# A four-layer graph kernel on one core: layer 3's product in two levels of Strassen with its factors streamed from DRAM, layer 2's sums kept in PSUM

## The chip, the core and the metric

The kernel runs on one core of a Trainium2 chip. The metric is device time in microseconds (us) of one launch; less is better. TensorE (PE) does the matrix products, VectorE (DVE), ScalarE (ACT) and GpSimd (POOL) the elementwise work, and every DMA is issued on SyncE's queue (SP).

## The reference

`x` is 128 graphs of 64 nodes with 512 features, in float32; `adj` is 128 matrices of 64x64. Four residual layers follow each other, `x = x + layer(relu(layernorm(x)))`. Cut to what is computed (h is the normed input, per graph):

```python
# layer 0: two hypergraph convolutions, 512 -> 1024 -> 512, with M = a 64x64 matrix made of adj
z = layer_norm(relu(rd * (M @ h) @ W1.T + b1)); y = rd * (M @ (z @ W2.T)) + b2 + h
# layer 1: attention weights from two dot products; one 512x512 product
out = (A @ h) @ w
# layer 2: attention, with q = h Wq, k = h Wk, v = h Wv (+ biases)
weight = adj * exp(q @ k.T); out = (weight / weight.sum(2)) @ v
# layer 3: three-hop diffusion; transition is 64x64
H = 0; Xk = h
for k in range(3):
    H = H + Xk @ Wk[k] + bk[k]
    Xk = transition @ Xk
out = relu(H)
```

Layer 3 is thus one product of the row block [h, T h, T T h] (1536 wide) with the three 512x512 matrices `Wk` under each other.

## The kernel before

**Tiles.** A group is 8 graphs, that is four tiles of 128 rows (t = 0 to 3); there are 16 groups. The first half of the run takes all groups through layers 0 and 1 and stores the result to a DRAM scratch (`xm`, L809). The second half loads it again (L344) and takes all groups through layers 2 and 3.

**The order.** Nothing is issued where it is written. Each helper (`pe`, `dve`, `act`, `pool`, `dma`) puts an operation with an engine, an assumed cost, the buffers it reads and writes and a priority into a graph (`Graph.op`, L52). `Graph.run` (L82) then plays the graph through with one clock for each engine and a fixed latency, picks on each engine the operation that can start first (the lower priority number among equals), gives out the buffers of `SLOTS` and `TWO` (L185 to L202), and at the end issues all operations in the order of the planned start. So the order on every engine is fixed when the program is built, and operations of several groups and layers are woven into each other. The priorities are the sum of a group's period (`PERIOD1`, `PERIOD2`), a shift for each part (`AT`, L281) and `step(us)` times a stretch for the layer (`STRETCH`, L280). Where the plan leaves PE idle for over 0.5 us, `fill` (L1011) puts in matmuls of ones.

**Strassen.** The large products are done two tiles at a time, as a 2x2 block product with seven block multiplications (Winograd's form). `strassen` (L589) makes the combinations of the left factor on DVE (`comb`, L599), `combine` and `combine_hT` (L384, L403) those of the weights, once. `seven` (L568) issues the seven products: product 1 is copied from PSUM to SBUF by ACT (L575), DVE adds products 6 and 7 to it (L577, L579), and products 2, 5, 4 and 3 are summed with these by an `emit` function of the layer. A float32 matmul is two passes on PE, so each matmul of the program is two records in the profile.

- Layer 2 (`layer2`, L811): the normed tiles are transposed to `hT`, DVE makes four combinations (L831), seven products of four 128x256 matmuls give q (with the product of Wq and Wk folded into one matrix `wg`), then logits (L879), exp, and seven more products give v; the biases of q and v are added by POOL (L866, L900) and DVE (L867, L902). L912 multiplies by the attention matrix, L918 adds to `x`.
- Layer 3 (`layer3`, L922): DVE and PE make the transition matrix and its square (L949, L959); for each pair of tiles (t0 = 0, 2) the left factor `a3` of 12 blocks is put together from a transposed h (L557) and the two products with the transition (L975, copied out by ACT at L980). Then `strassen` with 6 blocks of contraction and 256 columns: 42 matmuls of 128x256 for a pair, 84 for a group (PE at L607 with `wb_mem`). `emit_o` (L985) adds the bias on POOL (L989) and the result on DVE (L993, L994) and stores to `out` (L997).

The factors of `Wk` (all seven combinations) lie in SBUF for the whole second half, in `wb_mem` (10752 floats a partition), where `W2` and `w` lay in the first half; they are loaded (L1063) and combined (L393 to L396 with 1536 columns) at the change from the first to the second half.

Of the kernel before, what the change touches and what calls it, by code (L numbers as in the profile page):

```python
# [35 lines left out]
class Op:  # L36
    __slots__ = ("eng", "cost", "fn", "prio", "bufs", "npre", "succ", "ready", "seq")


class Graph:  # L40
# [11 lines left out]
    def op(self, eng, cost, fn, r=(), w=()):  # L52
        o = Op()
        o.eng, o.cost, o.fn, o.prio = eng, cost, fn, self.prio + self.shift
# [27 lines left out]
    def run(self, slots, after, fill):  # L82
# [22 lines left out]
        while left:  # L105
# [23 lines left out]
            if o.eng == "PE" and gap > 0.5 and since <= at["PE"]:  # L129
                fills.append((o.seq, slots["ps"][i], gap))  # L130
# [8 lines left out]
            end = t + o.cost + self.LATENCY[o.eng]  # L139
# [28 lines left out]
def tile_adj_preln_d4(  # L168
# [25 lines left out]
        ([("tmp", [P, D], 4), ("mB", [P, T, C + 1], 1)], [("s3", [P, 3, 6, P], 1)]),  # L194
        ([("z", [P, DH], 2)], [("hT", [P, KD, T * P], 1)]),
        ([("rT", [P, KH, P], 3)], [("vu", [P, 2, D + 1], 2), ("tt", [P, T, 2, C], 2)]),
        ([("s2", [P, 3, 4, P], 1), ("s1", [P, 3, 2, P], 2)], [("a3", [P, 3 * KD, P], 2)]),
        ([("y", [P, D], 2)], [("qT", [P, 2, 2 * P], 2)]),
        ([("mT", [P, KD, P], 3)], [("a3", [P, 3 * KD, P], 1)]),
        ([("row", [P, D], 4)], [("sh", [P, 4, 2, 2 * P], 1)]),  # L200
        ([("wa", [P, D], 1)], [("q", [P, D], 1)]),
    ]  # L202
# [29 lines left out]
    WB = const.tile([P, 10752], F32, name="wb_mem")  # L232
# [6 lines left out]
    w2_sb = view(WB, 0, KH, D)  # L239
    w2_x = view(WB, 4096, 3 * 4, D // 2).rearrange("p (i c) o -> p i c o", i=3)  # L240
    w_sb = view(WB, 7168, KD, D)
    w_x = view(WB, 9216, 3 * 2, D // 2).rearrange("p (i c) o -> p i c o", i=3)
# [4 lines left out]
    w3_sb = view(WB, 0, 3 * KD, D)  # L247
    w3_x = view(WB, 6144, 3 * 6, D // 2).rearrange("p (i c) o -> p i c o", i=3)

# [21 lines left out]
    def dma(kb, fn, r, w, issue=0.34):  # L271
        return G.op("SP", max(kb / 380.0, issue), fn, r, w)

    def quad(b):
        return b.t.rearrange("p (c k) -> p c k", c=4)

    FILL = 0.75


    STRETCH, PERIOD1, PERIOD2 = (2.11, 6.43, 4.5, 0.21), 79.8, 140.53  # L280
    AT = {  # L281
        "x0": -1458.56, "apart": 58.27, "w1": -1207.06, "b1": -1268.61, "w2": 312.2, "w": -214.25, "c1": 103.95,
        "l0": -1592.46, "c2": -560.69, "l1": 125.29, "c": 849.04, "g0": -1279.86, "g1": -1456.39, "g2": -589.08,
        "g3": -1259.16, "g": -1258.76, "bq": 321.93, "l3": 56.2, "wg": 1603.23, "w3": 387.13, "beg0": -72.8,
        "beg1": 73.58, "end00": 0.51, "end01": 19.09, "end11": -75.14, "new2": 31.64, "new3": 4.77, "end2": -39.58,
        "end3": -21.31, "load1": -108.19, "load2": 27.97, "m": 12.29, "h0": 9.53, "p0": 10.98, "z0": -29.14,
        "q0": 15.48, "y0": -518.61, "h1": -26.33, "p1": -22.59, "z1": -30.25, "q1": 4.48, "y1": -2.94, "s": -20.64,
        "t0": -25.67, "e0": -522.9, "t1": -42.32, "e1": -53.88, "hT": 8.77, "sh": 220.05, "lq": 8.14, "pt": -124.53,
        "v": 35.92, "pv": -915.5, "s3": 19.84, "tt": -865.12, "a0": 46.62, "b0": -371.48, "a1": 104.26, "b1_": 198.72,
# [46 lines left out]
    def load_group(g, src, apart=0.0):  # L336
        b = Buf("adj")
        dma(256, lambda: nc.sync.dma_start(b.t, adj[g]), [], [b])
        adjs[g] = b
        for t in range(T):  # L340
            xx = Buf("x")
            at, key = src(g, t)
            G.shift += apart
            dma(256, lambda xx=xx, at=at: nc.sync.dma_start(xx.t, at), key, [xx])  # L344
            xt[g, t] = xx
# [5 lines left out]
    def x_mid(g, t):  # L351
        return xmid[g, t], [("xmid", g, t)]
# [12 lines left out]
    load_w("w2", w2_sb, W2T)  # L365
    b2_b = load_row(b2)
    part("w")
    load_w("w", w_sb, w)
# [5 lines left out]
    bk3_b = const.tile([P, D], F32, name="bk3_b")  # L374
# [9 lines left out]
    def combine(name, w_, x_, kc, n, eng, olds=()):  # L384
# [7 lines left out]
        T1 = name + "T1"  # L392
# [38 lines left out]
    def setup_l0():  # L431
# [6 lines left out]
        pe(c_mm(512, KH), mm, ["gb2b", *wkeys("w2", 0, KH)], [p])  # L438
        act(0.6, lambda: nc.scalar.copy(row.t[0:1, :], p.t[0:1, :]), [p], [row])
        for c in range(KH):  # L440
            act(0.72, lambda c=c: nc.scalar.activation(w2_sb[:, c, :], w2_sb[:, c, :], AF.Copy, scale=gb2[:, 0, c:c + 1]), ["gb2g"], [("w2", c // 2)])
# [11 lines left out]
    def setup_l1():  # L453
        wa, a_b = Buf("col"), temp(a.partition_broadcast(P))
        for c in range(KD):
            dot(lambda c=c: w_sb[:, c, :], lambda: a_b.t, lambda c=c: wa.t[:, c:c + 1], [("w", c // 2), ("w", "given"), a_b], [(wa, c)])
# [36 lines left out]
    def setup_l3():  # L493
# [12 lines left out]
        dma(256, lambda: nc.sync.dma_start(bk3_b, bk3[0].partition_broadcast(P)), [], ["bk3"])  # L506
        for k in range(1, 3):
            b = temp(bk3[k].partition_broadcast(P))
            dve(0.69, lambda b=b: nc.vector.tensor_add(bk3_b, bk3_b, b.t), [b, "bk3"], ["bk3"])


# [39 lines left out]
    def transposed(src, ksrc, planes, back, kback, dst, kdst):  # L551
# [4 lines left out]
        dma(0, lambda: nc.sync.dma_start_transpose(u16(back()).rearrange("p (b r) -> p b r", r=P), u16(planes.t)), [planes], kback, 1.23)  # L556
        act(1.16, lambda: nc.scalar.copy(u16(dst()).rearrange("p c (k q) -> p c k q", q=2), u16(back()).rearrange("p (q c r) -> p c r q", q=2, c=KD)), kback, kdst)  # L557

    def proj(lhsT, rhs, p, r, first=True, last=True):
# [6 lines left out]
        pe(c_mm(512, k), mm, r if first else [*r, p], [p])  # L566

# [21 lines left out]
    def strassen(A, keys, B, kc, n, stag, emit):  # L589
# [11 lines left out]
        def prod(lhs, kl, b):  # L601
            rhs, kb = B[b]
# [18 lines left out]
    def scaled(dst, wdst, scale, ks, add, ka, p, u, v, n):  # L621
# [5 lines left out]
        dve(c_v(n, True), lambda: nc.vector.scalar_tensor_tensor(dst(), p.t[:, :n], scale(), add(), op0=ALU.mult, op1=ALU.add), [p, *ks, *ka], [wdst])  # L627

    def biased(dst, j, p, u, v, row, krow):
# [7 lines left out]
        dve(c_v(D // 2, True), lambda: nc.vector.tensor_add(dst.t[:, cols], p.t[:, :D // 2], add()), [p, ka], [(dst, j)])  # L637
# [494 lines left out]
```

## Time and profile before

| | |
|---|---|
| runs | 2374.16, 2375.67, 2378.42 us; median 2375.67 |
| profiled execution | 2372.54 us, of which the span of instructions is 2370.7 us |
| PE | busy 2343.9 us, 99% of the span, 12264 records |
| DVE | busy 1741.8 us, 73% |
| ACT | busy 1268.0 us, 53% |
| POOL | busy 955.9 us, 40% |
| DMA | 171.06 MB, 72 GB/s over the span |
| one group, first half (layers 0 and 1) | 71.7 us |
| one group, second half (layers 2 and 3) | 71.6 us (mean of nine) |

A line of the group table reads: source line, engine, operation, output from inputs, partitions by elements, count; then the busy time of all, the mean duration of one in ns, and the idle time ahead of them with what ended it. PE's matmuls are pipelined: a record lasts longer than the step from one start to the next, so the step is what a matmul costs in a dense stretch.

### The profile page before, as it was taken

The numbers are of one execution on the slowest core, as the hardware profiler recorded it, in microseconds if no ns is written. First come the engines' busy times: TensorE is split into PE (matmuls) and PEld (weight loads), VectorE is DVE, ScalarE is ACT, GpSimd is POOL, SyncE is SP. The second block draws the span as 40 slices with busy tenths as digits, with TensorE's granted clock in tenths as the row PEclk, the third lists the DMA queues.
The fourth block names the chain that finished last, engine by engine and source line by source line (L and its number), as shares of the span: only waits on it lengthen the run. The fifth ranks groups of instructions, "written<-read, shape, count | busy, mean of one in ns | idle before, by whom it ended". The sixth has DMA issues, their size and how long they took to land.

```text
span 2370.7 us, 34372 instructions
## 1 busy us (share of the span) xinstructions
PE 2343.9 (99%) x12264; PEld 1851.4 (78%) x12264; DVE 1741.8 (73%) x3798; ACT 1268.0 (53%) x1746; POOL 955.9 (40%) x1514
## 2 busy tenths in 40 slices
PE   9999999999999999999999999999999999999999
PEld 4677677776667776677788888888888888888887
DVE  7878778777778877777868566666666766667664
ACT  4566566566565676565745445444454444454422
POOL 6234555444555444555443323333323332323330
PEclk9999999999999999999999999999999999999999
DMA  7333233232232332232442322223222223222211
GB/s 259 79 80 60 53 69 69 72 80 54 54 74 65 76 73 48 67 69 70 125 120 59 76 66 60 68 49 72 73 63 69 55 56 78 70 63 63 52 37 41
DMA packets 336924, 171.06 MB, mean 72 GB/s; under 512 B 284656, under 2 KB 290672, under 8 KB 336752
## 3 DMA queue, kind: packets, MB, share of 16 engines
q1 hardware_dynamic: 336752, 168.86, 29.6%
q8 instruction: 96, 1.57, 0.3%
q14 instruction: 76, 0.62, 0.1%
HBM read 66.99 MB, written 34.70 MB: 43 GB/s over the span
## 4 chain that ended last, share of the span: by engine, by line
PE 85%; DVE 5%; DMA 4%; ACT 2%; issue 1%; POOL 1%; SPq 1%; DVEq 0%; ACTq 0%
PE ps L607 59%; PE ps L846 14%; PE ps L546 5%; PE ps L912 2%; PE ps L759 2%; PE ps L975 1%; PE ps L879 1%; DMA x<-xm 1%; DMA rw<-row 1%; DVE st L516 1%; DMA adj<-in_adj_dram 1%; POOL nm L524 0%; SPq L556 0%; DVE tmp_mB_s L599 0%; DVE o L381 0%
## 5 line engine op out<-in xcount | busy, mean ns | idle before, releaser
L537 ACT ACTIVATE h<-x,nm,rs 128x512 f32<-128x512 f32 x384 | 300.1, 810 | 402.6 <-POOL nm L524 369.9
L607 PE MATMUL ps<-wb_mem,s_s_a 128*128 128x256 f32 x2184 | 512.0, 380 | 1.0 <-DVE u L579 0.6
L607 PEld LDWEIGHTS ps<-wb_mem,s_s_a 128*128 128x128 f32 x2184 | 409.5, 190 | 74.7 <-issue 19.6
L518 POOL TENSOR_SCALAR rs<-mv 128x1 f32<-128x1 f32 x320 | 99.4, 311 | 494.8 <-DVE mv L517 479.3
L607 PE MATMUL ps<-wb_mem,tmp_mB_s 128*128 128x256 f32 x1152 | 262.5, 380 | 2.7 <-DVE tmp_mB_s L599 2.7
L607 PEld LDWEIGHTS ps<-wb_mem,tmp_mB_s 128*128 128x128 f32 x1152 | 218.1, 190 | 35.2 <-DVE tmp_mB_s L599 5.3
L607 PE MATMUL ps<-wa_mem,mT_a 128*128 128x512 f32 x512 | 238.8, 598 | 4.5 <-ACT mT_a L548 3.9
L607 PE MATMUL ps<-wb_mem,mT_a 128*128 128x256 f32 x1016 | 242.0, 380 | 0.0
L607 PE MATMUL ps<-wb_mem,rT_vu_tt 128*128 128x256 f32 x1024 | 238.3, 380 | 0.8 <-ACT rT_vu_tt L557 0.7
L607 PEld LDWEIGHTS ps<-wb_mem,rT_vu_tt 128*128 128x128 f32 x1024 | 192.4, 190 | 42.2 <-issue 14.0
L607 PEld LDWEIGHTS ps<-wb_mem,mT_a 128*128 128x128 f32 x1016 | 192.2, 190 | 31.8 <-issue 6.0
L516 DVE BATCH_NORM_STATS2 st<-x 128x6 f32<-128x512 f32 x256 | 173.5, 678 | 47.1 <-DMA x<-xm 42.1
L519 POOL TENSOR_TENSOR rs<-rs,mhalf 128x1 f32<-128x1 f32 x320 | 193.5, 605 | 26.4
L607 PEld LDWEIGHTS ps<-wa_mem,mT_a 128*128 128x128 f32 x512 | 97.8, 192 | 114.2 <-issue 103.2
L607 PE MATMUL ps<-wa_mem,s_s_a 128*128 128x512 f32 x384 | 180.6, 593 | 0.0
L989 POOL TENSOR_TENSOR u<-u,bk_b 128x256 f32<-128x256 f32 x96 | 76.1, 792 | 236.9 <-DVE u L579 168.3
L575 ACT COPY u<-ps 128x256 f32<-128x256 f32 (+1 forms) x160 | 72.7, 454 | 178.7 <-PE ps L846 106.9
L635 POOL TENSOR_TENSOR u<-u,row_sh 128x256 f32<-128x256 f32 x96 | 74.5, 784 | 227.8 <-DVE u L577 211.7
L734 ACT ACTIVATE z_hT<-z_hT 128x512 f32<-128x512 f32 x128 | 79.6, 627 | 156.2 <-DVE z_hT L627 156.2
L557 ACT COPY rT_vu_tt<-z_hT 128x1024 uint16<-128x1024 uint16 x128 | 147.2, 1160 | 15.7 <-DMA z_hT<-tmp_mB_s 15.3
L546 PEld LDWEIGHTS ps<-bd,h 128*128 128x128 f32 x1024 | 131.0, 192 | 26.3 <-issue 22.0
L524 POOL TENSOR_SCALAR nm<-mv,rs 128x1 f32<-128x1 f32 x320 | 136.1, 425 | 31.1
(174 smaller groups left out, 4303.7 us busy)
## 6 DMA issues: line engine op xcount, KB each, us to landing
x<-in_x_dram SPq DMA_DIRECT2D x64, 256.0 KB, 2.7
xm<-x SPq DMA_DIRECT2D x64, 256.0 KB, 2.1
x<-xm SPq DMA_DIRECT2D x64, 256.0 KB, 2.8
out_dram<-x SPq DMA_DIRECT2D x64, 256.0 KB, 2.1
adj<-in_adj_dram SPq DMA_DIRECT2D x32, 256.0 KB, 3.9
rw<-row SPq DMA_DIRECT2D x94, 64.0 KB, 2.6
wb_mem<-in_Wk_dram SPq DMA_DIRECT2D x6, 512.0 KB, 5.8
tmp_mB_s<-in_Wk_dram SPq DMA_DIRECT2D x8, 256.0 KB, 3.2
```

The costliest lines, as they stand in the source:

```text
L516: dve(0.69, lambda i=i: nc.vector.bn_stats(st.t[:, i, :], src(i)), [r[i]], [(st, i)])
L518: pool(0.32, lambda: nc.gpsimd.tensor_scalar_add(rs.t, mv.t[:, 1:2], EPS), [mv], [rs])
L519: pool(0.65, lambda: nc.gpsimd.tensor_tensor(rs.t, rs.t, mhalf, ALU.pow), [rs], [rs])
L524: pool(0.47, lambda: nc.gpsimd.tensor_scalar(nm.t, mv.t[:, 0:1], rs.t, -1.0, op0=ALU.mult, op1=ALU.mult), [mv, rs], [nm])
L537: act(0.82, lambda: nc.scalar.activation(h.t, xx.t, AF.Relu, bias=nm.t, scale=rs.t), [xx, nm, rs], [h])
L546: nc.tensor.matmul(quad(p)[:, c, :], h.t[:, c * P:(c + 1) * P], rhs(), start=True, stop=True)
L557: act(1.16, lambda: nc.scalar.copy(u16(dst()).rearrange("p c (k q) -> p c k q", q=2), u16(back()).rearrange("p (q c r) -> p c r q", q=2, c ...
L607: nc.tensor.matmul(p.t[:, :n], lhs()[:, c, :], rhs(c), start=first and c == 0, stop=c == kc - 1, skip_group_check=True)
L635: pool(0.75, lambda: nc.gpsimd.tensor_add(U.t[:, iv], U.t[:, iu], row()[:, cols]), [u, krow], [v])
L734: act(0.63, lambda: nc.scalar.activation(z.t[:, cols], z.t[:, cols], AF.Relu), [(z, j)], [(z, j)])
L846: nc.tensor.matmul(pair(p.t)[:, o, :], a, b, start=first and o == 0 and c == 0, stop=c == 1, skip_group_check=True)
L989: pool(0.88, lambda: nc.gpsimd.tensor_add(U.t[:, iv], U.t[:, u[1]], add()), [u, ka], [v])
```

## The change

1. **Layer 3's product** is taken for all four tiles of a group at once, as a 2x2 block product (Winograd's form) whose left blocks are pairs of tiles by half the features and whose seven multiplications are each done by a second level of seven: 7 x 7 products of three 128x128 matmuls, 147 for a group. The 49 factors of the weights are made on POOL in the first half (`setup_w3`, 21 pieces, one for each of the seven outer factors and three hops) and written to DRAM. In the second half each outer product loads its factors in two DMAs (four inner blocks, 768 KB, and three, 576 KB), 14 DMAs and 9408 KB for a group, into three buffers `wf`.
2. **Piling up in PSUM.** Each outer product runs in two PSUM banks (inner blocks 1, 2, 6, 5 in one, 7, 3, 4 in the other). Outer products 1, 6, 5, 3 add up in one chain of banks, 7, 4 in another; ACT copies the sum after each link to SBUF (`snapshot`, buffer `zz`), DVE adds in the other chain (`plus`), and POOL undoes the inner level with five adds (`emit`), then DVE does relu and the residual.
3. **Left factors.** DVE makes three inner combinations for each outer product (`xi`, 128x384), 21 for a group, and six outer ones (128x768), and four adds on h (128x256) ahead of the transposes.
4. **Layer 2** uses `chained` for `seven`: products 1, 6, 7, 4 pile up in one bank, 5 and 3 in another, ACT copies the sums out (for q with the bias), so that DVE's L577/L579 and POOL's L866 drop out there. The first half keeps `seven`.
5. **x in layer 2** is loaded a second time from `xm` for the residual, four DMAs of 256 KB more a group.
6. **Planner**: an operation can carry its own latency (3.2 us for transfers of the second half in place of 2.0), the fill threshold is 1.0 us in place of 0.5, and `STRETCH`, `PERIOD2` and most of `AT` have other values.

The core of the diff:

```diff
+    def chained(mul, U, n, emit, fifth=None, biased_by=None):
+        px, py, pz = (Buf("ps") for _ in range(3))
...
+        mul[1](px, True)
+        snap(px, (U, 0), 0)
+        mul[2](py, True)
+        emit(0, 0, py, (U, 0), (U, 0))
+        mul[6](px, False)
+        snap(px, (U, 1), 0)
+        mul[5](pz, True)
+        snap(pz, fifth)
+        mul[7](px, False)
+        snap(px, (U, 2), 1)
+        emit(1, 1, fifth, (U, 2), (U, 2))
+        mul[3](pz, False)
+        emit(0, 1, pz, (U, 1), (U, 1))
+        mul[4](px, False)
+        emit(1, 0, px, None, (U, 0))
...
+    def setup_w3(f, k, when):
...
+            b = Buf("wp")
+            dma(256, lambda: nc.sync.dma_start(b.t.rearrange("p (q n) k -> p q (n k)", q=2), src(i, j)), when, [b, *turn])
...
+            pool(1.3, lambda: sub(out.t, y.t, x_.t), [y, x_], [out])
...
+            pool(0.8, lambda: sub(R.t[:, 1:3], F.t[:, 1::2], F.t[:, 0:2]), [F], [R, *turn])
+            pool(0.53, lambda: sub(R.t[:, 0], F.t[:, 3], R.t[:, 1]), [F, R], [R])
+            pool(0.53, lambda: sub(R.t[:, 3], F.t[:, 2], R.t[:, 0]), [F, R], [R])
...
+            dma(256, lambda xx=xx, at=at: nc.sync.dma_start(xx.t, at), [*key, (PT, 0)], [xx, ("xo", g, t)], lat=LAT)
...
+                if t >= 2:
+                    dve(0.52, lambda hv=hv: nc.vector.tensor_add(hv()[:, 0], hv()[:, 0], hv()[:, 1]), [h], [h])
+                if t % 2:
+                    dve(0.52, lambda hv=hv: nc.vector.tensor_add(hv()[:, :, 0], hv()[:, :, 0], hv()[:, :, 1]), [h], [h])
...
+        def minus(y, x_, blk, kd):
+            for v in range(2):
+                dve(1.02, lambda v=v: nc.vector.tensor_sub(blk[v](), y[0][v](), x_[0][v]()), [*y[1][v], *x_[1][v]], [kd[v]])
...
+        def product(f, F, chain, first):
...
+            dve(0.6, lambda: sub(x2(), lo(B), lo(A)), [*ka, *kb], [(X, 0)])
+            dve(0.6, lambda: sub(x3(), hi(B), x2()), [*kb, (X, 0)], [(X, 1)])
+            dve(0.6, lambda: sub(x4(), hi(A), x2()), [*ka, (X, 0)], [(X, 2)])
...
+            for n in range(2):
+                w_, p, q = Buf("wf"), banks[chain][n], len(BLOCKS[n])
...
+                dma(q * 192, lambda n=n, w_=w_, q=q: nc.sync.dma_start(
+                    w_.t[:, :q].rearrange("p r k c -> p (r k c)"), fac[f - 1][n]), [("fac", f - 1, n, k, d) for k in range(3) for d in FACS[n]], [w_], lat=LAT)
...
+                        for k in range(3):
+                            nc.tensor.matmul(inner(p, q)[:, r, :], at()[:, k, :], w_.t[:, r, k, :], start=first and r == 0 and k == 0,
+                                             stop=k == 2, skip_group_check=True)
...
+        def emit(i, j, Z):
...
+            pool(0.84, lambda: add(z(0, 4, 3), z(0, 4, 3), bk3_b.t[:, 2 * j * P:2 * (j + 1) * P].rearrange("p (a b) -> p a b", a=2)), [(Z, 0), bk3_b], [(Z, 0)])
+            pool(0.92, lambda: add(z(1, 3), z(1, 3), cast(0)), [(Z, 0)], [(Z, 0)])
+            pool(0.92, lambda: add(z(0, 8, 7), z(3, 5), cast(2)), [(Z, 0), (Z, 1)], [(Z, 0), (Z, 1)])
+            pool(0.64, lambda: add(z(4, 5), z(7, 8), z(3, 4)), [(Z, 0), (Z, 1)], [(Z, 0), (Z, 1)])
+            pool(0.92, lambda: add(z(2, 4), z(5, 7), z(0, 8, 7)), [(Z, 0), (Z, 1)], [(Z, 0), (Z, 1)])
...
+        minus(S1, A00, S2[0], [k[0] for k in S2[1]])
+        product(1, A00, "X", True)
+        s0 = snapshot("X")
+        minus(A11, S2, A00[0], [k[-1] for k in A00[1]])
+        product(2, A01, "Y", True)
+        plus(s0, "Y")
+        emit(0, 0, s0)
+        product(6, S2, "X", False)
+        s1 = snapshot("X")
+        minus(A01, S2, A01[0], [k[-1] for k in A01[1]])
+        product(5, S1, "X", False)
+        s2 = snapshot("X")
+        product(3, A01, "X", False)
+        s3 = snapshot("X")
+        emit(0, 1, s3)
+        product(7, A00, "Y", True)
+        plus(s2, "Y")
+        emit(1, 1, s2)
+        product(4, A11, "Y", False)
+        plus(s1, "Y")
+        emit(1, 0, s1)
```

The order of the instructions that the planner gives out for the changed kernel can be listed without running it; the prediction uses this list for counts and for what stands next to what.

## Prediction

> **What bounds the kernel now.** I read the page's busy times first, then the slices and the chain of work that ended last, then windows of single groups of the second half.
>
> ```profile
> PE 2343.9 (99%) x12264; PEld 1851.4 (78%) x12264; DVE 1741.8 (73%) x3798; ACT 1268.0 (53%) x1746; POOL 955.9 (40%) x1514
> ...
> PE   9999999999999999999999999999999999999999
> ...
> PEclk9999999999999999999999999999999999999999
> ...
> PE 85%; DVE 5%; DMA 4%; ACT 2%; issue 1%; POOL 1%; SPq 1%; DVEq 0%; ACTq 0%
> PE ps L607 59%; PE ps L846 14%; PE ps L546 5%; PE ps L912 2%; PE ps L759 2%; PE ps L975 1%; PE ps L879 1%; DMA x<-xm 1%; DMA rw<-row 1%; DVE st L516 1%; DMA adj<-in_adj_dram 1%; POOL nm L524 0%; SPq L556 0%; DVE tmp_mB_s L599 0%; DVE o L381 0%
> ```
>
> PE is busy in every slice at the full clock, and 85% of the chain is PE, most of it L607, the Strassen products. So the end moves with PE's work, if the others keep it fed. How close they come is seen from three groups of the second half, cut at L959:
>
> ```profile
> core 0: us, PE busy (x) PEld busy (x) DVE busy (x) ACT busy (x) POOL busy (x), PEclk, DMA share, GB/s
> 1608.20:1679.50 71.30, 71.23 (x448) 62.07 (x444) 48.15 (x107) 33.91 (x47) 23.67 (x38) 1.00 0.28 65
> 1679.50:1751.70 72.20, 71.42 (x446) 61.91 (x442) 48.45 (x107) 33.73 (x47) 23.46 (x38) 1.00 0.27 65
> 1751.70:1823.30 71.60, 71.47 (x449) 62.16 (x445) 48.58 (x107) 34.31 (x48) 23.66 (x38) 1.00 0.29 65
> ```
>
> A group takes 71.6 us; PE waits 0.07, 0.78 and 0.13 us of it, a third of a microsecond on average. DVE is at 68%, ACT 47%, POOL 33%, DMA 28%. There is nothing to win by taking waits away, only by giving PE less work.
>
> **1. PE's work (the gain).** In the second half only layer 3's product changes for PE: 84 matmuls of 256 columns a group become 147 of 128 columns; in the list of instructions all other counts (layer 2, logits, L975) are the same. Each is two records: 168 become 294. The cost of a record is the step in a dense run. The nearest row for 128 columns with a new stationary operand each time is L546. From the timeline, two runs without gaps:
>
> ```profile
> 362.29 1.95 PE L546 MATMUL ps<-bd,h 128*128 128x128 f32 x16
> ...
> 1616.87 5.34 PE L607 MATMUL ps<-wb_mem,tmp_mB_s 128*128 128x256 f32 x24
> ```
>
> and from the groups by shape, the duration of one (in ns, the second number after the bar):
>
> ```profile
> L607 PE MATMUL ps<-wb_mem,tmp_mB_s 128*128 128x256 f32 x1152 | 262.5, 380 | 2.7 <-DVE tmp_mB_s L599 2.7
> ...
> L546 PE MATMUL ps<-bd,h 128*128 128x128 f32 x1024 | 131.9, 275 | 0.2 <-ACT bd L709 0.2
> ```
>
> A run lasts (n-1) steps and one duration: (1.95 - 0.275) / 15 = 0.1117 us for 128 columns, (5.34 - 0.38) / 23 = 0.2157 for 256. A group has 168 x 0.2157 = 36.24 us before and 294 x 0.1117 = 32.84 after: 3.40 less, over 16 groups **-54.4 us**. A Strassen level saves an eighth of the columns; half of that again is eaten by the step of 128 columns being a little over half that of 256.
>
> The Trainium skill speaks against this term: "TensorE: Matmul & The Clock Gate", section "Back-to-back issue gap", says that in a stream of weight loads and matmuls both set the spacing, about 81 ns at 128 columns where the formula for a lone matmul gives about 56. An estimate by that ratio, 1.45 times 0.1117, would make a group's product 47.6 us and the change 180 us slower. The L546 row already contains its weight loads, and the measurement decides.
>
> **2. PE's waits in the second half.** The work that takes over, by group, from the counts and the rows of before (256-wide DVE 0.42, 512-wide 0.68, 768-wide 0.95 undisturbed and 1.07 on average; 384-wide, not in the trace, between 0.42 and 0.68, I take 0.55; POOL 256-wide 0.79):
> - DVE loses L577/L579 of layer 2 and 3 (4 x 0.68 + 4 x 0.42), eight combinations (8 x 1.07), L993 (8 x 0.42): 16.3. It gains six combinations (6.4), 21 inner ones (11.6), four adds on h (1.8), six adds of chains (3 x 0.68 + 3 x 0.55 = 3.7): 23.5. Net +7.2: 48.4 becomes 55.6 of some 68 us, 82%.
> - ACT gains the copies of chains (six of 0.46, five of 0.58 for layer 2, eight of 0.46 to 0.58 for layer 3, less 1.9): +8, 42 us, 61%. POOL loses L866 and L989 (9.0) and gains 20 adds (14.6): 29 us, 43%.
> - DMA gains 9.63 MB of factors and 1.05 MB of x. At full share it moves 258 GB/s / 0.76 = 339 GB/s (first 60 us): +31.5 us on the 20 of today: 51 of 68 us, 76%.
>
> All stay under PE. That such a load can leave PE dense is shown by the first half: in 674 to 748 us DVE is at 79%, ACT at 61%, POOL at 50%, and PE is busy 74.0 of 74.0. New is that DVE's operations with two SBUF inputs meet more POOL work. Undisturbed they take 0.417 (256 wide), with a POOL operation under way up to 1.8:
>
> ```profile
> L599 DVE TENSOR_TENSOR s_s_a<-mT_a,s_s_a x74: 409/417/1796, 22.3 to 2261.2; 128x256 f32<-128x256 f32 x64, 128x768 f32<-128x768 f32 x10
> L599 DVE TENSOR_TENSOR mT_a<-mT_a x64: 409/418/954, 21.9 to 1221.7; 128x256 f32<-128x256 f32 x64
> ```
>
> In the timeline at 603.85 one lasts 0.95, to just after POOL's end. 31 such operations a group, 43% of them meeting POOL, waiting half of 0.79: +5.3 us, DVE at 61 of 68. Ends: nothing, or 31 x 0.79 = 24 us, which would put DVE at 80 us, over PE. I take 0.8 us more PE waits a group (the worst of the three windows as the rule): **+13 us**; ends 0 and +64 (4 a group, the whole gain and more).
>
> The piling up in PSUM adds a wait: the next product of a chain may start only when ACT has copied the sum out, and behind it PE's strict order waits. In layer 2 another product of 8 x 0.2157 = 1.73 us stands between, against 0.58 or 2 x 0.46 of ACT. In layer 3 the first bank is copied while the second bank's 18 records (2.0 us) run. Covered; if not, it is in the 64.
>
> **3. First half.** PE's work is the same. POOL gets 21 pieces of factors, 21 x (1.33 + 1.8) = 66 us on about 600 in 1190 us, SP 21 x 4 stores and 42 loads. In the list, groups 1 to 12 have another order than before, alternating in pairs. POOL's operations of 1.33 us stand ahead of the statistics (L518 to L524), for which ACT's L537 waits. There is slack: **+3 us**, ends -3 and +20.
>
> **4. Change-over and end.** Four combinations of 1536 columns (7.4 us of DVE) go, the first factor loads come; PE waits some 8 us there in all today: 0, ends -5 and +5. At the end, today DVE 0.42 + 0.43 and a store follow the last matmul; then it is a chain add of 0.55, three POOL adds of 0.5 to 0.79, two times 0.43: +2.7, and 1 us where the last group has no other work beside it (two places of dummy matmuls stand there in the list, as today): **+4 us**.
>
> **Sum.** -54.4 + 13 + 3 + 4 = -34.4 from the profiled 2372.5: 2338. The median of the runs lies 3.1 above the profiled one; with this **2341**.
>
> **Rivals.**
> - *The plan holds fully*, no new waits: 2341 - 16 = 2325, down to 2316 with the good ends of 3 and 4. For it: the first half's 74.0 of 74.0. Chance 0.15.
> - *DVE becomes the second bound*, its locks with POOL leaving PE waiting 2 us a group in place of 0.8: 2341 + 19 = 2360. For it: the 61 of 68. With the losses of 3 at their end, as far as no change. Chance 0.20, of which 0.05 within 0.2% of before (2371 to 2380).
> - *The factor stream comes late: slower.* Three buffers, 14 loads a group on one SP queue with eight transposes, nine loads and four stores. Between the first and last of the 147 matmuls the list has 46.6 us of PE work (32 matmuls of layer 2 among them), 3.3 us a load; a load is issued when its buffer is free, so it has two others' time, 6.7 us. Alone, 768 KB would take 2.1 us (256 KB, `xm<-x`) and 512 KB more at 339 GB/s, 3.7. In a full queue 512 KB took 5.8 and 1024 KB 8.9:
>
> ```profile
> xm<-x SPq DMA_DIRECT2D x64, 256.0 KB, 2.1
> ...
> wb_mem<-in_Wk_dram SPq DMA_DIRECT2D x6, 512.0 KB, 5.8
> ...
> wa_mem<-in_W1T_dram SPq DMA_DIRECT2D x2, 1024.0 KB, 8.9
> ...
> h<-o SPq DMA_TRANSPOSE x64, 3.1
> ```
>
>  With a transpose ahead (3.1) it is 6.8, just at the limit. The change loses all from 34.4 / (16 x 14) = 0.15 us of lateness a load; at 0.3 it is 2341 + 67 = 2408. Against it: the loads are spread out, the plan reckons the queue in, and L1063 and L312's rows were issued in bursts. Chance 0.19.
> - *The forecast*, 2326 to 2356: 0.46.
>
> Faster by over 0.2% (about what the runs can tell from no change): 0.15 + 0.15 + 0.46 = 0.76; within: 0.05; slower: 0.19. The range 2316 to 2385 leaves out most of the late stream and little below.
>
> **What would show it.** Right: the new product's records step by 0.112, a group of the second half takes 68 to 69.5 us, PE is near full in each, first half 71.7 a group. Wrong: PE or its weight loads waiting for the factors' DMA or for DVE's inner combinations a microsecond and more a group; a step of the 128-column records over 0.123 (294 x 0.123 = 36.2) would leave no gain at all.

## The result, and the profile after

The changed kernel took 2378.40 us, median of 12 runs (2366.5 to 2383.4), against 2375.36 for the kernel before, also 12 runs (2372.3 to 2378.4): ratio 1.0009, 95% interval 0.9995 to 1.0023. That is no change where 2341 us and "faster" were forecast. The profiled execution took 2374.24 us, the one of before 2372.54.

The page of the changed kernel; the rows are those shown of before, with the DMA slices added:

```profile
PE 2306.3 (97%) x14288; PEld 1872.0 (79%) x14288; DVE 1933.0 (81%) x4000; ACT 1386.7 (58%) x1986; POOL 1190.1 (50%) x1777
...
PE   9999999999999999999999999999999999999998
...
DMA  7333233333434433233436787777797877788666
...
PE 59%; DVE 14%; DMA 13%; ACT 6%; POOL 5%; issue 3%; SPq 1%; DVEq 0%; POOLq 0%; ACTq 0%
PE ps L678 26%; PE ps L1107 12%; PE ps L916 12%; PE ps L579 4%; DMA h<-o 3%; DMA w2m_wm_a_wf<-fac 3%; DMA rw<-row 2%; DVE st L549 2%; POOL rs L552 1%; PE ps L830 1%; DVE rT_vu_tt L1022 1%; DVE o L382 1%; POOL nm L557 1%; PE ps L1053 1%; ACT h L570 1%
```

PE's busy time fell by 37.6 us and the span rose by 1.8. The chain tells why: PE held 85% of it before and 59% now; DVE went from 5% to 14%, DMA from 4% to 13%. The slices still say 9 everywhere, since a tenth hides a wait of 5%. The DMA row has two levels, 3 in the first half and 7 to 8 in the second.

Three groups of the second half, cut at the transition's square as before (columns as there):

```profile
1641.16:1711.74 70.58, 68.50 (x568) 63.19 (x567) 58.99 (x119) 41.63 (x61) 33.43 (x49) 1.00 0.80 218
1711.74:1780.77 69.03, 68.26 (x568) 63.19 (x567) 59.92 (x119) 41.39 (x61) 34.71 (x49) 1.00 0.78 223
1780.77:1850.61 69.84, 67.99 (x568) 63.04 (x567) 58.45 (x119) 41.65 (x61) 33.97 (x49) 1.00 0.79 220
```

PE idles 2.1, 0.8 and 1.9 us of a group, against 0.07, 0.78 and 0.13. DVE at 59 us, ACT at 41.6 and DMA at 79% are near the 55.6 to 61, 42 and 76% of the prediction; POOL's 34 lies above its 29. So the loads of the engines were reckoned well in the main, and PE waits all the same.

What PE waits for from 1400 to 2250 us (three of five rows: total us, times, longest), with the transfers of that stretch (KB each, median us to landing):

```profile
PE ps L1107 <- DMA w2m_wm_a_wf<-fac: 10.3, 16, 2.0
PE ps L985 <- DVE rT_vu_tt L970: 6.9, 12, 1.1
PE ps L916 <- ACT z_hT L590: 4.8, 5, 1.5
```

```profile
w2m_wm_a_wf<-fac SPq DMA_DIRECT2D x84, 768.0 KB, 5.0
w2m_wm_a_wf<-fac SPq DMA_DIRECT2D x84, 576.0 KB, 5.2
x<-xm SPq DMA_DIRECT2D x96, 256.0 KB, 3.8
out_dram<-x SPq DMA_DIRECT2D x49, 256.0 KB, 4.0
...
wa_q<-o SPq DMA_TRANSPOSE x49, 4.8
h<-o SPq DMA_TRANSPOSE x48, 5.0
```

The kernel before, in the same stretch:

```profile
out_dram<-x SPq DMA_DIRECT2D x46, 256.0 KB, 2.1
x<-xm SPq DMA_DIRECT2D x46, 256.0 KB, 2.8
...
h<-o SPq DMA_TRANSPOSE x48, 3.1
```

The new product (L1107) waits for its factors; layer 2's (L916) waits for ACT's L590, which writes the transposed `hT`. The transposes take 4.8 to 5.0 us where they took 3.1, the stores 4.0 where they took 2.1, and the loads of x 3.8 where they took 2.8.

**Where the time went.** I split the trace's PE starts into work (each shape's median step) and waits (the rest). Work is 2304.3 us before and 2251.2 after, 53.1 less. Waits are 61.0 and 113.0, 52 more. What follows the last matmul is 4.4 and 7.2. The sum, -53.1 + 52 + 2.8 = +1.7, is the difference of the profiled executions. By place: layer 0 of the last group ends (its last product, L759 before, L830 after) at 1185.7 us before and at 1210.4 after, 24.7 later with the same matmuls of the layers and 4.3 us more of dummy ones; from there to the last matmul it is 1180.6 and 1154.9, so 25.7 is won of the 53.1, and 27.4 goes to new waits. These split further. Counted from the starts again, with dummy matmuls as waits, the part up to the first group's last transition product (L975 before, L1053 after) waits 15.7 us before and 8.0 after, and all that follows it 32.5 before and 68.4 after. So the change-over won some 8 us and the groups behind it lost 36 (28 in sum, against the 27.4 of the other count).

### The profile page after: what moved, and what is told of

The parts are those of the page before. It is cut to its first block, busy times and chain, and to the rows that moved or that the text cites. A ratio compares the mean times of both kernels' runs of the same rounds, so it can differ in the third digit from the quotient of the medians.

```text
span 2372.5 us, 39872 instructions
## 1 busy us (share of the span) xinstructions
PE 2306.3 (97%) x14288; PEld 1872.0 (79%) x14288; DVE 1933.0 (81%) x4000; ACT 1386.7 (58%) x1986; POOL 1190.1 (50%) x1777
## 3 DMA queue, kind: packets, MB, share of 16 engines
q1 hardware_dynamic: 408176, 357.30, 55.6%
## 4 chain that ended last, share of the span: by engine, by line
PE 59%; DVE 14%; DMA 13%; ACT 6%; POOL 5%; issue 3%; SPq 1%; DVEq 0%; POOLq 0%; ACTq 0%
PE ps L678 26%; PE ps L1107 12%; PE ps L916 12%; PE ps L579 4%; DMA h<-o 3%; DMA w2m_wm_a_wf<-fac 3%; DMA rw<-row 2%; DVE st L549 2%; POOL rs L552 1%; PE ps L830 1%; DVE rT_vu_tt L1022 1%; DVE o L382 1%; POOL nm L557 1%; PE ps L1053 1%; ACT h L570 1%
## 5 line engine op out<-in xcount | busy, mean ns | idle before, releaser
L1107 PE MATMUL ps<-w2m_wm_a_wf 128*128 128x128 f32 x2304 | 299.7, 276 | 10.2 <-DMA w2m_wm_a_wf<-fac 9.4
L1107 PEld LDWEIGHTS ps<-w2m_wm_a_wf 128*128 128x128 f32 x2304 | 279.8, 192 | 17.2 <-issue 6.5
L678 PE MATMUL ps<-w2m_wm_a_wf,s_s_zz 128*128 128x256 f32 x1152 | 278.8, 382 | 7.8 <-DVE s_s_zz L670 5.6
L1107 PE MATMUL ps<-w2m_wm_a_wf,tmp_mB_xi 128*128 128x128 f32 x2016 | 264.2, 275 | 2.5 <-DMA w2m_wm_a_wf<-fac 1.5
L678 PEld LDWEIGHTS ps<-w2m_wm_a_wf,s_s_zz 128*128 128x128 f32 x1152 | 216.8, 191 | 60.2 <-issue 19.8
L1107 PEld LDWEIGHTS ps<-w2m_wm_a_wf,tmp_mB_xi 128*128 128x128 f32 x2016 | 246.9, 192 | 6.3 <-issue 2.7
L678 PE MATMUL ps<-w2m_wm_a_wf,rT_vu_tt 128*128 128x256 f32 x1024 | 238.8, 380 | 2.3 <-ACT rT_vu_tt L590 2.2
L678 PE MATMUL ps<-wa_mem,mT_sx 128*128 128x512 f32 x512 | 236.4, 593 | 0.7 <-ACT mT_sx L581 0.6
L678 PEld LDWEIGHTS ps<-w2m_wm_a_wf,rT_vu_tt 128*128 128x128 f32 x1024 | 192.3, 190 | 46.5 <-issue 14.8
L678 PE MATMUL ps<-wa_mem,s_s_zz 128*128 128x512 f32 x384 | 180.3, 595 | 4.3 <-DVE s_s_zz L670 3.8
L557 POOL TENSOR_SCALAR nm<-mv,rs 128x1 f32<-128x1 f32 x320 | 146.0, 457 | 30.2
L590 ACT COPY rT_vu_tt<-z_hT 128x1024 uint16<-128x1024 uint16 x128 | 147.2, 1159 | 16.9 <-DMA z_hT<-tmp_mB_xi 16.2
L579 PEld LDWEIGHTS ps<-bd,h 128*128 128x128 f32 x1024 | 130.4, 193 | 30.6 <-issue 12.2
L579 PE MATMUL ps<-bd,h 128*128 128x128 f32 x1024 | 133.1, 277 | 7.3 <-DVE bd L859 7.1
```

What stands on the lines that cost most here:

```text
L557: pool(0.47, lambda: nc.gpsimd.tensor_scalar(nm.t, mv.t[:, 0:1], rs.t, -1.0, op0=ALU.mult, op1=ALU.mult), [mv, rs], [nm])
L579: nc.tensor.matmul(quad(p)[:, c, :], h.t[:, c * P:(c + 1) * P], rhs(), start=True, stop=True)
L678: nc.tensor.matmul(p.t[:, :n], lhs()[:, c, :], rhs(c), start=first and c == 0, stop=c == kc - 1, skip_group_check=True)
L1107: nc.tensor.matmul(inner(p, q)[:, r, :], at()[:, k, :], w_.t[:, r, k, :], start=first and r == 0 and k == 0, stop=k == 2, skip_group_check ...
```

## The experiments

Two losses are to be explained. For the first half (24.7 us) theory A is POOL's factor operations, B the other order of the list, C the factors' loads and stores. For the second half (27.4 us) theory D is the factor stream, E the port that DVE and POOL share. Ratios are to the kernel before on the same chip; its median was 2370.4 to 2375.4 us on the chips used, so times of different runs compare to some 5 us, and ratios better. The end of layer 0 scatters too: the changed kernel and the runs s1, s2, s3, d1 and d2, which have the same first half, reach it at 1204.8 to 1210.4 us. "Waits" are PE's waits per group from 1400 to 2200 us, from the starts as above: 1.82 us before, 4.02 in the changed kernel.

One more number goes with each run: where the planner's own clock ends, that is the length of the plan as the program itself reckons it (the value that `Graph.run` returns). It is 2354.9 for the kernel before and 2329.4 for the changed one.

### First half: operations, order or transfers

**f1_no_pool**: `sub(...)` of the 84 factor operations of POOL becomes nothing. The order is not quite the same: the stores now read `F`, the planner's clock ends at 2331.2, and PE's order differs from its record 744 on.

```diff
-            pool(1.3, lambda: sub(out.t, y.t, x_.t), [y, x_], [out])
+            pool(1.3, lambda: None, [y, x_], [out])
```

> Leaves out: the 84 POOL operations that make the factors (the factors stored are the plain blocks of Wk, so layer 3's product is another one). Same order on every engine, same DMAs. Theory A (the POOL operations themselves cost the first half: they stand ahead of the statistics and hold DVE up at the shared port): the first half goes from 73.5 us a group back to about 71.9, the whole is 20 to 25 us under the changed kernel, 2352 to 2358. Theory B (the other order in which the planner puts the first half costs it): no change, 73.3 to 73.6 a group, 2374 to 2382. Theory C (the 42 loads and 84 stores of 512-byte pieces do): no change here.

Measured: 2372.49 us, ratio 1.0002 (0.9988 to 1.0015); layer 0 ends at 1207.5 us, 73.6 a group. That is 2.9 us under the changed kernel's profiled execution and within the scatter. As the order is another one, this run alone doesn't settle A; the next one, in exactly the changed kernel's order, does.

**f2_no_factor_work**: also no loads and stores for the factors; the second half's loads read `Wk` itself, the same bytes. Same order.

```diff
-            dma(256, lambda: nc.sync.dma_start(b.t.rearrange("p (q n) k -> p q (n k)", q=2), src(i, j)), when, [b, *turn])
+            dma(256, lambda: None, when, [b, *turn])
```

> Leaves out: all of the factor work in the first half, POOL operations, loads and stores; the second half loads as many bytes in as many pieces from Wk itself (so layer 3's product is another one). Same order on every engine. Theory A: as without the POOL operations alone, 71.9 us a group, 2350 to 2358. Theory B: no change, 73.3 to 73.6. Theory C: 71.9 here, but 73.5 in the run that keeps the DMAs.

Measured: 2370.98 us, ratio 1.0005 (0.9991 to 1.0019); layer 0 ends at 1202.0 us, 72.9 a group. The work with its transfers is 8.4 us against the changed kernel's execution and 2.8 against the earliest of the six; 16.3 stay with no factor work at all. So A and C together are the smaller part, how they share it isn't shown, and B is suspected. A group of the second half took 71.3 us, 0.7 more, though its loads have the same bytes; why is open.

**f0_old_order**: as f2, with one piece alone put into the planner's graph. The planner then gives all groups from the second on one order, nearly that of before; the second half's order is that of the changed kernel.

```diff
-        for i in range(2 * g, min(2 * g + 2, 21)):
+        for i in range(0, 1 if g == 0 else 0):
```

> The factor work is planned for one piece alone, so that the planner falls back into one steady order for every group of the first half, nearly that of the kernel before; as in the run without factor work nothing is computed, loaded or stored for the factors, and the factor loads of the second half read Wk itself (wrong values, same bytes). The second half's order is that of the changed kernel. Theory B (the alternating order costs the first half some 16 us): 71.7 us a group in the first half, layer 0 of the last group ends at 1186 to 1190 us in place of 1202 (no factor work, alternating order), the whole 2352 to 2358 us. Rival B2 (something else of the change costs it: the planner's new latency and fill values, the new pools): 72.5 us a group or more, layer 0's end at 1200, the whole 2368 to 2372 us.

Measured: 2359.15 us, ratio 0.9951 (0.9936 to 0.9965); layer 0 ends at 1191.3 us, 72.0 a group. B holds: 10.7 of the 24.7 us go with the order alone (f0s1 below, with the same first half, ends it at 1187.4, 14.6 under f2). The planner's clock ends at 2317.2, 12.2 earlier, so this part of the loss stood in the plan. 5.6 us against before (1185.7) remain: 3.1 of them arise in the third group and 3.5 in the last four, while the groups between run at about 71.7 us as before. What costs them there isn't shown.

PE's waits from 150 to 1180 us; first the changed kernel (two of its eight rows, 16.0 us in all), then f0 (two of three, 5.5):

```profile
PE ps L579 <- DVE bd L859: 6.6, 6, 2.3
PE ps L678 <- DVE s_s_zz L670: 4.4, 10, 0.6
```

```profile
PE ps L678 <- DVE s_s_zz L670: 3.0, 4, 1.4
PE ps L579 <- DVE bd L859: 2.3, 2, 1.3
```

In the kernel before these waits are not there; its two rows in that stretch sum to 1.0 us. In the alternating order PE meets the attention matrix (L859) and the combinations (L670) before DVE has them.

**c1_factors_in_gaps**: the factor work hidden from the planner and issued in POOL's longest empty stretch of 12 groups; the two rows of `c3_b` made later, as their memory serves as a buffer.

```diff
+        for t, fn in extra:
+            o = Op()
+            o.fn, o.tag, o.eng, o.cost, o.seq = fn, None, None, 0.0, len(self.ops) + len(order)
+            order.append((t, o.seq, o))
```

> All of the computation is done. The factor work is hidden from the planner and put afterwards into POOL's longest empty stretch of each of 12 groups, so that the planner gives one steady order from the second group on (a third order, neither that of before nor the alternating one); the second half as in the changed kernel. Theory B (alternating order): 71.8 to 72.3 us a group in the first half, layer 0's end at 1190 to 1196 us, the whole 2358 to 2366 us. Rival A2 (the factor work itself with its loads and stores costs it wherever it stands): 73 us a group or more, the whole 2370 to 2376 us. If this third order is itself a bad one, it is also 73 us a group, but then the groups 14 and 15, which have no factor work, are as slow as the others.

Measured: 2406.79 us, ratio 1.0153 (1.0128 to 1.0178); 74.7 us a group, 74.0 in the last ones. Inconclusive on the work: the third order is bad by itself, as the last groups, which have no factor work, are nearly as slow, and the planner's clock ends at 2363.0, 33.6 after that of the changed kernel. It speaks for B all the same: by PE's matmuls, this order is that of two groups of the changed kernel, which take 74.9 and 73.9 us there, while its fourteenth group, in f0's steady order by PE's matmuls, takes 71.7.

**c2_factors_steady**: exactly f0's order, with the real factor work put into POOL's planned empty stretches of 3 us and more. The outer combinations follow from each other, so that 12 subtractions and 21 loads do for 21 and 42; the bias rows of layers 2 and 3, which use the same memory, are loaded after it.

```diff
+                for m, (i, j, f) in enumerate(chain):
+                    sp_at(t, load(1 if m else 0, k, i, j))
+                    t += 6.0
+                    if f == 6:
+                        t = pool_at(t, lambda: sub(F, F, R)) + 0.5
+                    elif m:
+                        t = pool_at(t, lambda: sub(F, R, F)) + 0.5
```

> All of the computation is done. The planner gives exactly the order of the run 'old order' (one steady order, the factor work unplanned), and the factor work (all but the first piece) is put afterwards into POOL's planned empty stretches of 3 us and more, 12 subtractions and 21 loads in place of 21 and 42 because the outer combinations follow from each other, the bias rows of layers 2 and 3 loaded after it. Theory B (the alternating order costs some 11 us of the first half, the work itself some 8): between the run 'old order' (2359 us) and 8 more, 2359 to 2367 us, 72.0 to 72.6 us a group in the first half. Rival A2 (the work disturbs any order, as 74.7 us a group in the third order may say): 73.5 us a group or more, 2375 us or more.

Measured: 2362.41 us, ratio 0.9956 (0.9942 to 0.9971); layer 0 ends at 1193.5 us, 72.2 a group. B again: the work is done and the first half ends 2.2 us after f0's. Over the runs with the same first half (c2, c2d1, e1, e2: 1189.1 to 1196.0; f0, f0s1, without the work: 1187.4 and 1191.3) it costs some 4 us. This kernel beats both.

### Second half: stream or port

**s1_no_stream**: factor loads only in groups 0 and 1, later groups use what lies in the buffers; same order.

```diff
-                dma(q * 192, lambda n=n, w_=w_, q=q: nc.sync.dma_start(
+                dma(q * 192, lambda n=n, w_=w_, q=q: g < 2 and nc.sync.dma_start(
```

> Leaves out: the factor loads from the third group of the second half on (28 of 224 are left; the products use what lies in the buffers). Same order otherwise. Theory D (the stream makes the second half wait: its own lateness, and the transposes and x loads behind it): PE's waits in a group of the second half fall from 4.1 us to about 2, the group from 70.6 to about 68.5, the whole 25 to 30 us under the changed kernel, about 2350. Theory E (DVE, which is at 84% with its waits for POOL at the port): PE's waits stay above 3.4 us, the group above 69.8, the whole falls by under 12 us.

Measured: 2343.89 us (2343.0 to 2347.1), ratio 0.9884 (0.9869 to 0.9898); 68.4 us a group, waits 1.83, the transposes at 3.1 and 3.3 us. D holds: from layer 0's end to the last matmul it takes 1124.7 us, 30.2 less than in the changed kernel; the new waits of the second half are gone. Of the row L985 above 5.2 of 6.9 us stay, so that wait is hardly the stream's.

**s3_no_pool_emit**: the 320 adds of POOL in layer 3's `emit` do nothing.

```diff
-            pool(0.92, lambda: add(z(1, 3), z(1, 3), cast(0)), [(Z, 0)], [(Z, 0)])
+            pool(0.92, lambda: None, [(Z, 0)], [(Z, 0)])
```

> Leaves out: the five POOL adds of each block of layer 3 that undo the inner level (320 in all; the output of layer 3 is another one). Same order otherwise. Theory E: DVE's operations with two SBUF inputs get back to their undisturbed time, DVE falls from 59 to about 56 us a group, PE's waits from 4.1 to under 3, the whole 15 to 20 us under the changed kernel. Theory D: DVE gets shorter, PE's waits stay at 3.7 and above, the whole falls by under 7 us.

Measured: 2370.35 us, ratio 0.9994 (0.9982 to 1.0006); 70.0 us a group, 0.6 less; PE's waits 3.4, between what E (under 3) and D (3.7 and above) said. E is minor.

**s2_sixth_bytes**: all loads stay, each moves a sixth of its bytes from the third group on.

```diff
-                    w_.t[:, :q].rearrange("p r k c -> p (r k c)"), fac[f - 1][n])
+                    w_.t[:, :q].rearrange("p r k c -> p (r k c)")[:, :q * (384 if g < 2 else 64)], fac[f - 1][n][:, :q * (384 if g < 2 else 64)])
```

> The changed kernel with all 14 factor loads of a group in their places, but from the third group on each moves only a sixth of its bytes (the rest of the buffer keeps old values). Order and number of instructions are those of the changed kernel. Theory D1 (the bytes of the stream cost the second half: a load takes 5 us in a queue shared with everything else): close to the run without the stream, 2343 to 2350 us, 68.4 to 68.8 us a group. Rival D2 (not the bytes but the load itself: its place in the SP queue, its wait for a free buffer and its fixed latency): 2362 to 2374 us, 69.8 us a group or more.

Measured: 2342.34 us, ratio 0.9887 (0.9871 to 0.9904). D1: the bytes, not the loads or their waits in the queue. Three groups of it, and what its transfers took from 1400 to 2250 us:

```profile
1627.99:1696.16 68.17, 67.73 (x568) 62.97 (x567) 59.18 (x119) 41.47 (x61) 35.07 (x49) 1.00 0.45 107
1696.16:1764.36 68.20, 67.76 (x567) 63.00 (x566) 60.75 (x119) 41.25 (x61) 34.76 (x49) 1.00 0.44 108
1764.36:1833.17 68.81, 68.00 (x567) 63.04 (x567) 59.29 (x119) 41.57 (x61) 35.15 (x49) 1.00 0.47 107
```

```profile
x<-xm SPq DMA_DIRECT2D x100, 256.0 KB, 3.7
out_dram<-x SPq DMA_DIRECT2D x50, 256.0 KB, 2.3
w2m_wm_a_wf<-fac SPq DMA_DIRECT2D x85, 128.0 KB, 2.4
...
wa_q<-o SPq DMA_TRANSPOSE x50, 3.1
h<-o SPq DMA_TRANSPOSE x48, 3.5
```

DVE, ACT and POOL do what they do in the changed kernel and the DMA share is 0.45 in place of 0.79. The group takes 68.2 us, the transposes are near 3.1 again (3.1 and 3.5) and the stores near 2.1 (2.3). The loads of x are not: 3.7 us here, 3.6 in s1, as in the changed kernel. By line, the second load of each tile (L981), which the change adds, takes 3.9 us here and in the changed kernel alike; the first (L346) takes 2.7 here, 3.3 in the changed kernel, and 2.85 in the kernel before (L344).

**f0s1_both**: f0's and s1's edits together.

> Both together: the steady order without factor work in the first half, and factor loads only in the first two groups of the second (wrong values). If the two causes B and D are separate and make up all of the lost gain: 2374 less 20 to 24 (first half) less 28 (second half), 2320 to 2328 us, about what the plan would have given by the PE work alone (2325 in the rival 'the plan holds fully'). If they overlap (what is saved in one place is waited for in another): 2335 us or more.

Measured: 2327.59 us, ratio 0.9819 (0.9805 to 0.9834), at the upper end of what was expected. The two losses are separate: against the changed kernel's 1.0009, f0's ratio is lower by 0.0058 and s1's by 0.0125, which add up to 0.0183, and with both it is lower by 0.0190. In time, f0 gains some 14 us and s1 some 30.

### How the bytes act: late for their own buffer, or in the way of others

**d1_half_buffers, d2_single_buffers, c2d1_both**: six buffers of two inner blocks, or twelve of one, in the memory of the three; 28 or 49 loads a group, each issued earlier before its use.

```diff
-        ([("w2m", [P, 7168], 1), ("wm", [P, 3584], 1)], [("a3", [P, 3, KD, P], 4), ("wf", [P, 4, 3, P], 3)]),
+        ([("w2m", [P, 7168], 1), ("wm", [P, 3584], 1)], [("a3", [P, 3, KD, P], 4), ("wf", [P, 2, 3, P], 6)]),
...
+                halves = [Buf("wf") for _ in range(0, q, 2)]
+                for e, w_ in enumerate(halves):
+                    m = min(2, q - 2 * e)
+                    dma(m * 192, lambda n=n, w_=w_, m=m, e=e: nc.sync.dma_start(
```

> All of the computation is done. Layer 3's three factor buffers of four inner blocks become six of two in the same memory, each outer product's two loads become four (28 a group); a buffer comes free after two inner products, and five others lie between its release and its use, by the 46.6 us in 49 inner products some 8.3 us in place of 6.7. The planner gives the second half another order; the first half is the changed kernel's. Theory D1a (the bytes make a single load land too late for its buffer's turn): 69.0 to 69.9 us a group in the second half, the whole 2354 to 2366 us. Rival D1b (the bytes delay everything else in the one queue, the transposes and x first, and more loads only add to the queue): 70.4 us a group or more, 2370 us or more.

> All of the computation is done. As the half buffers, but twelve buffers of one inner block, 49 loads of 192 KB a group; eleven others lie between release and use, some 10.5 us. Theory D1a: 68.6 to 69.6 us a group, the whole 2348 to 2362 us. Rival D1b: SP issues 49 loads of 0.32 us in place of 14 (11 us a group more of the queue), each waiting for its buffer with transposes behind it: 70.6 us a group or more, 2372 us or more.

> All of the computation is done. The factors put into POOL's empty stretches of the steady order, and the half buffers. If B and D1a hold and the gains add: 2374 less 6 to 14 less 8 to 19, 2342 to 2358 us, faster than both kernels. If neither holds: 2370 us or more.

Measured: 2469.34 (ratio 1.0409, 1.0393 to 1.0424), 2481.62 (1.0463, 1.0448 to 1.0479) and 2458.02 us (1.035, 1.033 to 1.037). All three missed, and they tell nothing of D1: with the priorities tuned for 14 loads, the planner made a plan that ends at 2416.3, 2429.0 and 2404.1 on its own clock, with 36, 27 and 36 places of dummy matmuls in place of 10. They are PE work without use; d1 from 1400 to 2250 us has a row that the changed kernel doesn't have there:

```profile
L1178 PE MATMUL ps<-ones 128*128 128x128 f32 x470 | 57.2, 277 | 0.0
```

**e1_half_short_plan, e2_half_late_plan, e3_half_later_plan**: the half buffers with c2's first half, and the second half's numbers in `STRETCH`, `PERIOD2` and `AT` chosen anew until the planner's clock ends near where it did for the changed kernel and c2: 2307.4, 2319.8 and 2327.4. They differ in the landing time that the planner reckons for a factor load, 3.2, 4.3 and 4.8 us.

```diff
-    STRETCH, PERIOD1, PERIOD2 = (2.11, 6.43, 41.882, 4.8895), 79.8, 148.89
+    STRETCH, PERIOD1, PERIOD2 = (2.11, 6.43, 41.882, 4.466), 79.8, 150.636
```

> All of the computation is done. The first half is that of 'factors steady' (2362 us). The six half buffers of the failed run, but with the second half's priorities chosen anew, so that the planner's own clock ends at 2307 us with 13 places of dummy matmuls (the failed run: 2416 with 36; factors steady: 2317 with 10); the planned latency of a factor load stays 3.2 us. What lay between the planner's clock and the chip so far: 11 to 15 us without the stream's bytes, 42 to 45 with them. Theory D1a (a load lands too late for its own buffer's turn, so that 1.6 us more of lead helps): 15 to 33 between plan and chip, 2322 to 2340 us. Rival D1b (the bytes delay transposes and other loads as well, and lead doesn't help): 42 us or more, 2349 us or more.

> As the one before, but the planner reckons 4.3 us for a factor load, which is what it took on the chip with half buffers; its clock ends at 2320 us, 12 places of dummies. Theory D1a: the planner knows of the lateness, 13 to 22 us between plan and chip, 2333 to 2342 us. Rival D1b: 42 us or more, 2362 us or more.

> As the one before with 4.8 us for a factor load; the planner's clock ends at 2327 us, 13 places of dummies. Theory D1a: 12 to 18 us between plan and chip, 2339 to 2345 us, so that nothing is gained over 4.3. Rival D1b: 42 us or more, 2369 us or more.

Measured: e1 2350.25 us (ratio 0.9895, 0.9878 to 0.9911), e2 2359.99 (0.9935, 0.992 to 0.995), e3 2379.35 (1.0026, 1.0015 to 1.0037). By the totals D1b holds: 43, 40 and 52 us lie between plan and chip, about as with three buffers (e2's 40 is 2 under what D1b said). The trace says more. e1 from 1400 to 2250 us, PE's waits (three of its seven rows) and the transfers:

```profile
PE ps L973 <- ACT z_hT L647: 5.4, 10, 1.0
PE ps L1168 <- ACT s_s_zz L1177: 2.7, 3, 1.1
...
PE ps L1168 <- DMA w2m_wm_a_wf<-fac: 0.3, 1, 0.3
```

```profile
w2m_wm_a_wf<-fac SPq DMA_DIRECT2D x254, 384.0 KB, 4.4
x<-xm SPq DMA_DIRECT2D x99, 256.0 KB, 4.2
...
wa_q<-o SPq DMA_TRANSPOSE x50, 4.2
h<-o SPq DMA_TRANSPOSE x48, 4.5
```

PE's waits for the factors (L1168 here) are nearly gone, 10.3 us become 0.3, and the waits per group fall from 4.25 (c2) to 3.11. Layer 2's product (L973 here) still waits for the transposed h, whose transposes take 4.2 to 4.5 us. Both ways are seen with the bytes alone changed, in s2. In the changed kernel the steps into and within the new product lose 1.4 us a group where s2 loses 0.1, those into layer 2's product 0.5 against 0.1, and those within the attention product (L985) 0.1 more. From c2 to e1 the steps into and within the new product fall from 1.5 to 0.6 us a group and those of the attention product from 1.2 to 0.4, while those of layer 2's product rise from 1.0 to 1.55; as the second half's order is another one too, the lead alone isn't shown to do this. e1 is 1.05% faster than the kernel before, and more against the changed one; how much of that is its shorter plan and how much its lead isn't separated.

## Why the prediction was wrong

One table puts the runs in order: the planner's clock, the measured median, and what lies between (the runs are from several chips, so this holds to some 5 us).

| kernel | plan | measured | between |
|---|---|---|---|
| before | 2354.9 | 2375.4 | 20 |
| after | 2329.4 | 2378.4 | 49 |
| s1, s2 (few bytes) | 2329.4 | 2343.9, 2342.3 | 14, 13 |
| f0s1 (few bytes, steady order) | 2317.2 | 2327.6 | 10 |
| f0, c2 (steady order) | 2317.2 | 2359.2, 2362.4 | 42, 45 |
| e1, e2, e3 (half buffers) | 2307.4, 2319.8, 2327.4 | 2350.3, 2360.0, 2379.4 | 43, 40, 52 |

With the stream some 40 to 50 us lie between plan and chip, without it 10 to 20. The plan itself is 12 us longer in the alternating order. Two steps of the prediction failed, the waits of the second half and those of the first, each by over 20 us.

1. **PE's work, -54.4: right.** Measured -53.1; the new product's records step by 112 ns, as the L546 row had said, and far from the spacing that would have made the change 180 us slower. One remark there is wrong: of the eighth that a Strassen level saves, 4.53 us a group, the step of the narrower records eats 1.13, a quarter and not half.
2. **PE's waits in the second half, +13: failed.** Measured +36 behind the change-over, by the starts 1.82 us a group before and 4.02 after. The +13 was 0.8 us a group, set by the worst window of the kernel before, and checked against busy shares; the shares came out as worked out (DVE 59 us, DMA 79%). It was set by PE's busy time, which shows 0.07 to 0.78 us of waits where the starts show 1.82. And what PE waits for is not a full engine: s1 and s2, with DVE at the same 59 us and few factor bytes, win back some 30 us. With all the bytes the landing grew for the transposes (3.1 to 4.9) and the stores (2.1 to 4.0), and a load of factors took 5.0 to 5.2, where it was reckoned at 3.7 alone. I reckoned the lateness of the factors alone, and only as a rival. The transposes I didn't reckon at all, though layer 2's product stands behind them. The piling up in PSUM was nearly covered, as said: from 1400 to 2250 us ACT's copies (L1116) hold PE's weight loads up for 3.8 us and its matmuls not at all.
3. **First half, +3 with "there is slack": failed.** Measured +24.7, beyond its end of +20. By the profiled executions, 10.7 of this is the order (f2 to f0), 8.4 the factor work with its transfers (changed kernel to f2), and 5.6 stay open; with the scatter of these ends, the order is some 11 to 15 and the work some 3 to 8. I had seen in the list that the groups alternate and gave it no price.
4. **Change-over and end, +4:** the tail grew by 2.8 us, forecast 2.7. The change-over, put at 0 with an end of -5, won some 8 us; this hides a part of the error in 2.
5. **Rivals.** "The factor stream comes late" had a part of the mechanism at half its price. The bytes cost some 30 us over 224 loads, 0.13 us a load, where 0.15 was the point at which the gain is gone; I took 0.3 for the case and gave it 0.19. But of this only some 1.4 us a group, 0.10 a load, is lost at the new product; the rest is lost behind the transposes and the attention product. The landing lay between the 3.7 alone and the 6.8 with a transpose ahead. "DVE becomes the second bound" was wrong: its inner combinations took the 0.55 us assumed (below), it filled 59 of 70 us, and without POOL's adds a group was 0.6 us shorter. (The 1.8 us that the prediction gives for a 256-wide operation beside POOL's is of a 768-wide one in the same row; the longest 256-wide one of L599 took 1.49.) "The plan holds fully" was met, 2327.6 for 2325, only by f0s1, which leaves out the factor work and most loads.

```profile
L1090 DVE TENSOR_TENSOR tmp_mB_xi<-w2m_wm_a_wf x96: 524/549/1626, 1292.9 to 2352.3; 128x384 f32<-128x384 f32 x96
```

## What to carry to other kernels

When a change replaces resident data by a stream, reckon not only whether its loads come in time but what its bytes do to the landing of other transfers on the queue, above all those with a product waiting behind them. A change of the order by a list scheduler is a cost of its own: compare the scheduler's own end of plan for both versions, and for the part that was not meant to change. An engine at 99% whose neighbours are all under 85% can still lose 2 us a group to latency.

## What was not expected of the hardware

At a DMA share of 0.78, 217 GB/s, the landing grew for some transfers and not for others: from the kernel before (0.27, 63 GB/s) the transposes went from 3.1 to 4.8 and 5.0 us, the 256 KB stores from 2.1 to 4.0, the first loads of x from 2.85 to 3.3, and the loads of `adj` from 2.7 only to 2.8. At 0.44, 107 GB/s (s2), the transposes took 3.1 and 3.5 and the stores 2.3. The changed kernel spans 16.9 us in 12 runs, the kernel before 6.1. That this comes of the stream isn't shown: in four runs each, c2 and f0 with the stream span 5.9 and 6.0, and s1, s2 and f0s1 with few bytes 4.0, 5.8 and 6.0.
